# Filter rows of a spatially varying 3x3 filter made four times, in four groups of partitions

## The chip, the cores and the metric

The kernel runs on one NeuronCore of one Trainium2 chip. The metric is the device time of one execution in microseconds (us). All data are 32-bit floats. In the profile PE is TensorE, PEld its loading of weights, DVE is VectorE, ACT is ScalarE, POOL is GpSimd, and SP is the engine that issues most DMAs.

## The reference, cut to what matters

Eight images of 64 channels and 64x64 pixels go through four layers: a convolution block with attention over all pixels (layer 0), two blocks of shifted-window attention with an MLP (layer 1), a filter whose nine taps are computed from the data (layer 2), and a selective state-space scan in four directions with a normalisation and a multi-scale block behind it (layer 3). The change lies in layer 2:

```python
def filter_norm(f, axis):
    m = jnp.mean(f, axis=axis, keepdims=True)
    sd = jnp.std(f, axis=axis, keepdims=True, ddof=1)
    return (f - m) / (sd + 1e-10) * STD          # STD = sqrt(2)/3

s = jnp.einsum('bchw,tc->bthw', x, sw) + sb[None, :, None, None]
s = filter_norm(s, axis=1)                       # nine values per pixel
...
cf = filter_norm(cf, axis=2)                     # nine values per channel
xp = jnp.pad(x, ((0, 0), (0, 0), (1, 1), (1, 1)))
out = jnp.zeros_like(x)
for idx in range(9):
    i, j = idx // 3, idx % 3
    out = out + xp[:, :, i:i+H, j:j+W] * s[:, idx:idx+1] * cf[:, :, idx, None, None]
a = jnp.where(out >= 0, out, 0.1 * out)
y = conv_general_dilated(a, w2, (1, 1), ((0, 0), (4, 4)), ...)   # 1x9 along a row
return x + y + b2
```

## The kernel before, in words

Two images at a time lie on the 128 partitions (64 channels each), with their 4096 pixels along the free dimension, in eight chunks of 512 pixels (`NCH = 8`, `CH = 512`). So there are four pairs of images.

The program (`tile_kernel`, end of the listing) first runs the front of pair 0 alone: layers 0, 1, 2 and the inputs of the scan (`_Direct.front`). Then `scans(p, ...)` runs the scans of pair p, and beside them, in small portions, the back of pair p-1 and the front of pair p+1. Those portions are Python generators: each `yield` carries a cost written by hand (2.3 for a tap of layer 2, 14 for the end of a chunk), and after every scan step as many portions are drawn as keep the front in step with the scans. After the fourth pair's scans its back runs alone. The order of the instructions in each engine's queue is fixed when the program is built; an engine takes its instructions in that order and waits where a semaphore asks for it. A second path (`_Net.layer0` to `layer3`) handles inputs out of range and isn't entered with these data; it shares some constants with the first.

A scan step is: two DMAs that spread rows of B and C over the partitions; one product on POOL (L1687); two exponentials on ACT (L1707) into PSUM; two scans on DVE (L1710); the products with C on POOL (L1721, or L1723 with half of them on DVE, L1724); and two matmuls with the identity on PE (L1737), of two passes each, that add the result to `y`. The product tile `v` has six buffers, so POOL's L1687 of a later step waits until the matmuls L1737 of an earlier one have read it.

Layer 2 in the first path (L1501 to L1551) does this for every chunk:

- L1515: one matmul turns the 128 channel rows into `p_m`, 18 rows (nine centred filter values for each of the two images). L1517 squares them on ACT, L1519 sums the squares over nine with a matmul (`var9`), L1522 to L1525 make 1/(sd + 1e-10) on ACT with logarithms and exponentials, and L1527 makes the filter rows `f` on DVE, 18 partitions by 512.
- For each of the nine taps, L1532 is a matmul with an 18x128 table (`pick`) that spreads the two rows of this tap over the 128 partitions (`pb`, a PSUM bank); L1535 on DVE multiplies the shifted image by the channel's filter value and by `pb` (`tap`, three buffers); L1536 adds it to `acc` with an identity matmul over all 128 rows.
- L1542 and L1543 apply the leaky ReLU, L1546 does the 1x9 convolution as nine matmuls into `py`, and L1549 adds the result to X.

Every 32-bit matmul appears as two weight loads and two passes in the trace, so one tap is two passes of L1532 and two of L1536. `acc` and `py` share one PSUM bank (tag `acc`, `bufs=1`), so the `acc` of the next chunk starts only when L1549 has read `py`, while up to three `pb` and `tap` of that chunk can be made ahead. Banks for `pb`, `p_m` and `p_v` come from a pool of three, or from two pools in turn while the front of pair 0 runs alone (`bank`, L1179).

The constants are packed on the host (`_pack`) into six arrays. `load` (L239) fetches an array with one DMA on ACT's queue: arrays 0 and 1 at the start, 2 (`TEMP`) for a moment during `prepare`, 5 (`TABLES`, the tables of layer 2, first 18 rows only) at the start of every layer 2. `prepare` (L308 to L316) multiplies `swbd` by `cen9` to get `swc`, and `cen9` by `sb` to get `sbc`. `channel_filters` (L802) uses the table `cw2T` in 36 small passes (L818) once per layer 2 and gives the channel's filter values `cf`.

Of the kernel before, what the change touches and what calls it, by code (L numbers as in the profile page):

```python
# [9 lines left out]
F32 = mybir.dt.float32  # L10
AF = mybir.ActivationFunctionType
ALU = mybir.AluOpType
# [66 lines left out]

GENERAL = ("xpT", "dtT", "alog", "rpb0", "rpb1", "maskh", "maskv", "norm1_b0", "norm1_b1", "qb0", "qb1", "kb0", "kb1", "vb0", "vb1", "pb0", "pb1", "f1b0", "f1b1", "norm2_b0", "norm2_b1", "smask")
TEMP = ("swbd", "ds")
TABLES = ("cw2T", "pick")
TEMPW = ("xr", "drT", "alogs", "rpbT0", "rpbT1", "maskq", "b_all", "smask_t")


def _pack(w):
# [62 lines left out]
    e9 = np.eye(TAPS, dtype=np.float32)  # L151
    put("swbd", _blockdiag(f["sw"]))
    put("sb", _dup(_col(f["sb"])))
    put("cen9", _blockdiag(e9 - np.float32(1.0 / TAPS)))
    put("var9", _blockdiag(np.full((TAPS, TAPS), 1.0 / (TAPS - 1), np.float32)))
    put("cw1T", _dup(f["cw1"].T))
    mid = f["cw1"].shape[0]
    put("cb1", _col(f["cb1"]))
    put("cw2T", f["cw2"].reshape(C, TAPS, mid).transpose(2, 1, 0))
    pick = np.zeros((2 * TAPS, TAPS, P), np.float32)  # L160
    for im in range(2):
        for t in range(TAPS):
            pick[TAPS * im + t, t, 64 * im : 64 * im + 64] = np.sqrt(2.0) / 3
    put("pick", pick)
    put("cb2", _dup(f["cb2"].reshape(C, TAPS)))
    put("gmask", np.repeat(np.eye(2, dtype=np.float32) / L, 64, axis=0))
    w2 = f["w2"][:, :, 0, :]
# [41 lines left out]
    temp = [x for x in items[n_first:] if x[0] in TEMP]  # L209
    tempw = [x for x in items[n_first:] if x[0] in TEMPW]  # L210
    keep = [x for x in items[n_first:] if x[0] not in GENERAL + TEMP + TEMPW + TABLES]
    tables = [(n, sh, a[0 : 2 * TAPS]) for n, sh, a in items if n in TABLES]
    packs, layout = [], []
    for g, part in enumerate((items[:n_first], keep, temp, tempw, late, tables)):
        packs.append(np.ascontiguousarray(np.concatenate([x[2] for x in part], axis=1)))
# [10 lines left out]
class _Net:  # L226
# [45 lines left out]
    def prepare(self):  # L272
        nc, w, const = self.nc, self.w, self.const
        self.eps = const.tile([P, 5], F32, name="eps", tag="eps")
        for i, e in enumerate((LN_EPS, CN_EPS, BN_EPS, 1e-37, 1e-10)):
            nc.gpsimd.memset(self.eps[:, i : i + 1], e)
        eps_bn = self.eps[:, 2:3]

        bn1 = w["bn1"]
        sc = const.tile([P, 2, C], F32, name="bn1sc", tag="bn1sc")  # L280
        self.bn_fold((sc[:, 0, :], sc[:, 1, :]), bn1[:, 0, :], bn1[:, 1, :], bn1[:, 2, :], bn1[:, 3, :], eps_bn)
        self.w1a = const.tile([65, C], F32, name="w1a", tag="w1a")
        nc.vector.tensor_tensor(self.w1a[0:64, :], w["w1T"][0:64], sc[0:64, 0, :], ALU.mult)
        nc.vector.tensor_copy(self.w1a[64:65, :], sc[64:65, 1, :])

        self.w1bd = const.tile([P, P], F32, name="w1bd", tag="w1bd")
        nc.gpsimd.memset(self.w1bd, 0.0)
        for im in range(2):
            lo = slice(64 * im, 64 * im + 64)
            nc.vector.tensor_tensor(self.w1bd[lo, lo], w["w1T"][lo], sc[lo, 0, :], ALU.mult)  # L290
        self.b1row = const.tile([1, 2, C], F32, name="b1row", tag="b1row")
        nc.vector.tensor_copy(self.b1row, sc[0:1, 1, :].unsqueeze(1).to_broadcast([1, 2, C]))
        self.ones = const.tile([P, P], F32, name="ones", tag="ones")
        nc.gpsimd.memset(self.ones, 1.0)
        self.sums = const.tile([P, B // 2, 2, 32], F32, name="sums", tag="sums")

        bn = w["bn23"]
        self.bn23 = const.tile([P, 4], F32, name="bn23", tag="bn23")
        for i in range(2):
            self.bn_fold(  # L300
                (self.bn23[:, 2 * i : 2 * i + 1], self.bn23[:, 2 * i + 1 : 2 * i + 2]),
                *[bn[:, 4 * i + k : 4 * i + k + 1] for k in range(4)],
                eps_bn,
            )

        nr = 2 * TAPS

        self.swc = const.tile([P, nr], F32, name="swc", tag="swc")  # L308
        self.sbc = const.tile([nr, 1], F32, name="sbc", tag="sbc")
        with self.tc.tile_pool(name="psf", bufs=1, space=PSUM) as ps:  # L310
            pw = ps.tile([P, nr], F32, name="pswc", tag="pswc")
            nc.tensor.matmul(pw, lhsT=w["swbd"], rhs=w["cen9"], start=True, stop=True)
            nc.scalar.activation(self.swc, pw, AF.Copy)
            pb = ps.tile([nr, 1], F32, name="psbc", tag="psbc")
            nc.tensor.matmul(pb, lhsT=w["cen9"], rhs=w["sb"], start=True, stop=True)
            nc.scalar.activation(self.sbc, pb, AF.Copy)  # L316
        self.dsum = const.tile([P, 1], F32, name="dsum", tag="dsum")
        nc.vector.tensor_reduce(self.dsum, w["ds"], AX.X, ALU.add)
# [523 lines left out]
    def layer2(self, X):  # L842
# [5 lines left out]
        with ExitStack() as st:  # L848
# [7 lines left out]
            for c in range(NCH):  # L856
                cols = slice(c * CH, (c + 1) * CH)

                pm = ps.tile([nr, CH], F32, name="ps_m", tag="mm")
                nc.tensor.matmul(pm, lhsT=self.swc, rhs=X[:, cols], start=True, stop=True)  # L860
                q = wk.tile([nr, CH], F32, name="q2", tag="q2")
                nc.scalar.activation(q, pm, AF.Square, bias=self.sbc)
                pv = ps.tile([nr, CH], F32, name="ps_v", tag="pv")
                nc.tensor.matmul(pv, lhsT=w["var9"], rhs=q, start=True, stop=True)

# [3 lines left out]
                nc.scalar.activation(d, d, AF.Ln, bias=self.eps[0:nr, 4:5])  # L869
                nc.scalar.activation(d, d, AF.Exp, scale=-1.0)  # L870
                f = wk.tile([nr, CH], F32, name="f2", tag="f2")
                nc.vector.scalar_tensor_tensor(f, pm, self.sbc, d, ALU.add, ALU.mult)

                acc = ps.tile([P, 8, 64], F32, name="acc", tag="acc", bufs=1)
                for t in range(TAPS):
# [272 lines left out]
class _Direct:  # L1148
# [352 lines left out]
    def layer2(self, X):  # L1501
        nc, tc, w, net = self.nc, self.tc, self.w, self.net
        XP = self.padded("XP")
        for c in range(NCH):
            nc.scalar.activation(self.rows(XP, c), self.img(X[:, c * CH : (c + 1) * CH]), AF.Copy)
            yield 1
        nr = 2 * TAPS
        with tc.tile_pool(name="w2", bufs=2) as wk:
            net.load(wk, (5,))
            cf = net.channel_filters(X, wk, self.pf, "f")  # L1510
            for c in range(NCH):
                x = X[:, c * CH : (c + 1) * CH]

                pm = self.bank("p_m", (nr, CH))
                nc.tensor.matmul(pm, lhsT=net.swc, rhs=x, start=True, stop=True)  # L1515
                q = wk.tile([nr, CH], F32, name="q2", tag="q2")
                nc.scalar.activation(q, pm, AF.Square, bias=net.sbc)  # L1517
                pv = self.bank("p_v", (nr, CH))
                nc.tensor.matmul(pv, lhsT=w["var9"], rhs=q, start=True, stop=True)  # L1519

                d = wk.tile([nr, CH], F32, name="d2", tag="d2")
                nc.scalar.activation(d, pv, AF.Ln, bias=net.eps[0:nr, 3:4])  # L1522
                nc.scalar.activation(d, d, AF.Exp, scale=0.5)
                nc.scalar.activation(d, d, AF.Ln, bias=net.eps[0:nr, 4:5])
                nc.scalar.activation(d, d, AF.Exp, scale=-1.0)  # L1525
                f = wk.tile([nr, CH], F32, name="f2", tag="f2")
                nc.vector.scalar_tensor_tensor(f, pm, net.sbc, d, ALU.add, ALU.mult)  # L1527

                acc = self.total("acc", (P, 8, 64))
                for t in range(TAPS):  # L1530
                    pb = self.bank("pb", (P, 8, 64))
                    nc.tensor.matmul(pb, lhsT=w["pick"][:, t, :], rhs=f, start=True, stop=True)  # L1532
                    src = XP[:, 8 * c + t // 3 : 8 * c + t // 3 + 8, t % 3 : t % 3 + 64]
                    tap = wk.tile([P, 8, 64], F32, name="tap", tag="tap", bufs=3)
                    nc.vector.scalar_tensor_tensor(tap, src, cf[:, t : t + 1], pb, ALU.mult, ALU.mult)  # L1535
                    nc.tensor.matmul(acc, lhsT=w["ident"], rhs=tap, start=(t == 0), stop=(t == TAPS - 1))  # L1536
                    yield 2.3
                a = wk.tile([P, 8, 72], F32, name="act", tag="act")
                nc.vector.memset(a[:, :, 0:4], 0.0)
                nc.vector.memset(a[:, :, 68:72], 0.0)  # L1540
                t1 = wk.tile([P, 8, 64], F32, name="t1", tag="t1", bufs=1)
                nc.scalar.activation(t1, acc, AF.Copy)  # L1542
                nc.vector.scalar_tensor_tensor(a[:, :, 4:68], acc, 0.1, t1, ALU.mult, ALU.max)  # L1543
                py = self.total("py", (P, 8, 64))
                for t in range(TAPS):
                    nc.tensor.matmul(  # L1546
                        py, lhsT=w["w2bd"][:, t, :], rhs=a[:, :, t : t + 64], start=(t == 0), stop=(t == TAPS - 1)
                    )
                nc.vector.scalar_tensor_tensor(  # L1549
                    self.img(x), py, w["b2"], self.img(x), ALU.add, ALU.add  # L1550
                )  # L1551
                yield 14
# [336 lines left out]
```

## Time and profile before

| what | value |
|---|---|
| median of 3 runs | 14022.91 us |
| lowest and highest | 14009.71 and 14023.95 us |
| the profiled execution's own time | 14012.53 us |
| its span, first to last instruction | 14010.7 us |
| mean granted TensorE clock | 0.862 |
| PE, DVE, ACT, POOL busy | 11364.2, 8425.0, 7041.2, 8178.9 us |
| PE's passes of L1532, all | 576, 331.6 us |
| PE's passes of L1536, all | 576, 403.5 us |
| layer 2 of pair 0 (alone), from its first L1532 to its last L1549 | 1409.5 to 1732 us |
| layer 2 of pairs 1, 2, 3 (beside scans) | 4081 to 4468, 7295 to 7659, 10654 to 11017 us |

A row of the groups and of the timeline has the line of the kernel, the engine, the operation, output<-inputs, shapes, and how often; times are in us, mean durations in ns. In the timeline the first two columns are start and length, and neighbouring instructions of one kind are merged ("x6" is six of them). The passes of a matmul overlap at their ends, so the distance from start to start says what a pass costs, rather than its own length. The table of windows gives, for each stretch, its length, then the busy time of PE, PEld, DVE, ACT and POOL (with the number of instructions), the granted TensorE clock (1.00 is full), the share of the DMA engines and GB/s.

### The profile page before, as it was taken

What the parts mean: (1) busy time and instruction counts of PE and PEld (TensorE: products, weight loads), DVE (VectorE), ACT (ScalarE), POOL (GpSimd) and SP (SyncE); (2) the same over time, 40 slices, a digit from 0 to 9 for tenths busy, and PEclk for the clock granted to TensorE, in tenths of its full rate; (3) what the DMA queues carried; (4) which work ended last, traced back from release to release, by engine and by line L of the source; (5) the groups of instructions that cost most, each with busy time, mean ns of one, the idle gap of its engine ahead of it and who ended that gap; (6) DMA issues with size and microseconds to landing.
All of it is one profiled execution on the core that took longest, in us unless ns stands there. A gap on an engine that the chain in (4) does not pass through costs nothing. (4 is left out here: it accounts for less than half of the span.)

```text
span 14010.7 us, 141613 instructions
## 1 busy us (share of the span) xinstructions
PE 11364.2 (81%) x46358; PEld 4240.7 (30%) x46358; DVE 8425.0 (60%) x9763; ACT 7041.2 (50%) x15460; POOL 8178.9 (58%) x4111
## 2 busy tenths in 40 slices
PE   9888979978888669988889667997998866666665
PEld 2255222234433222224433222223443222222221
DVE  0222254477766874356675767337666677997875
ACT  5533156556544645555553645555554554454442
POOL 0000046578767765556665685457666688878982
PEclk9966789989889789998899788998888878888887
DMA  0000044456555754445554675335544577878882
GB/s 17 1 1 2 6 163 162 159 185 226 195 181 189 246 195 149 135 154 176 176 177 160 227 248 172 131 132 189 173 163 166 183 253 259 273 250 275 276 273 97
DMA packets 705499, 2379.23 MB, mean 170 GB/s; under 512 B 81060, under 2 KB 81188, under 8 KB 703980
## 3 DMA queue, kind: packets, MB, share of 16 engines
q1 hardware_dynamic: 681024, 2315.57, 48.9%
q10 hardware_dynamic: 23724, 54.50, 1.0%
q8 instruction: 367, 6.01, 0.2%
q14 instruction: 384, 3.15, 0.1%
HBM read 2269.08 MB, written 100.66 MB: 169 GB/s over the span
## 5 line engine op out<-in xcount | busy, mean ns | idle before, releaser
L1687 POOL TENSOR_TENSOR vd<-B,du 128x1024 f32<-128x1024 f32 x2048 | 4841.8, 2369 | 3920.1 <-DMA B<-rows 2103.0
L1737 PE MATMUL yd<-vd,pack 128*128 128x512 f32 x8192 | 4625.9, 695 | 1265.4 <-POOL vd L1721 449.5
L1710 DVE TENSOR_TENSOR_SCAN hd<-dad,carry,vd 128x512 f32<-128x512 f32 x2464 | 3093.2, 1271 | 1146.2 <-ACT dad L1707 669.9
L1707 ACT ACTIVATE dad<-du,As 128x512 f32<-128x512 f32 x4096 | 2718.4, 680 | 1017.3 <-DVE hd L1710 701.9
L1737 PEld LDWEIGHTS yd<-vd,pack 128*128 128x128 f32 x8192 | 1624.1, 215 | 3956.6 <-issue 1863.1
L1721 POOL TENSOR_TENSOR vd<-hd,C 128x1024 f32<-128x1024 f32 x768 | 1811.7, 2359 | 1324.0 <-DVE hd L1710 695.7
L1723 POOL TENSOR_TENSOR vd<-hd,C 128x512 f32<-128x512 f32 x1280 | 1637.0, 1280 | 317.9 <-DVE hd L1710 230.0
L1277 ACT ACTIVATE e<-s 128x512 f32<-128x512 f32 x2048 | 1199.2, 591 | 1030.1 <-PE s L1271 1028.6
L1710 DVE TENSOR_TENSOR_SCAN dad<-dad,carry,vd 128x512 f32<-128x512 f32 x1120 | 1427.6, 1275 | 126.5 <-POOL vd L1687 77.5
L1271 PE MATMUL s<-X 64*128 64x512 f32 x4096 | 1343.5, 647 | 105.5 <-ACT e L1277 105.3
L1263 PE MATMUL po<-e,VT 128*64 128x512 f32 x4096 | 1155.4, 631 | 19.0 <-ACT e L1277 19.0
L1718 ACT ACTIVATE carry<-hd 128x1 f32<-128x1 f32 (+1 forms) x1792 | 357.3, 201 | 1225.9 <-DVE hd L1710 1215.5
L1724 DVE TENSOR_TENSOR vd<-dad,C 128x512 f32<-128x512 f32 x1280 | 860.9, 673 | 72.7 <-ACT carry L1718 62.4
L1425 PEld LDWEIGHTS w_av<-vals,w_e 64*64 64x64 f32 x16384 | 630.9, 163 | 204.5 <-ACT w_e L1415 99.4
L1425 PE MATMUL w_av<-vals,w_e 64*64 64x9 f32 x16384 | 658.6, 218 | 38.2 <-ACT w_e L1415 38.0
L1271 PEld LDWEIGHTS s<-X 64*128 64x128 f32 x4096 | 363.5, 187 | 1052.4 <-issue 823.7
L1710 DVE TENSOR_TENSOR_SCAN hd<-dad,vd 128x512 f32<-128x512 f32 x352 | 420.1, 1211 | 191.7 <-ACT dad L1707 88.3
L1748 DVE TENSOR_TENSOR Y<-Y,yd 128x512 f32<-128x512 f32 x128 | 124.8, 975 | 661.3 <-PE yd L1737 661.1
L1718 ACT ACTIVATE carry<-dad 128x1 f32<-128x1 f32 x1120 | 189.5, 169 | 616.6 <-DVE dad L1710 614.4
L1415 ACT ACTIVATE w_e<-w_e 128x512 f32<-128x512 f32 x512 | 310.8, 627 | 360.7 <-DVE w_e L1410 239.4
L1410 DVE TENSOR_TENSOR w_e<-w_s,bias 128x512 f32<-128x512 f32 x512 | 328.8, 682 | 236.3 <-PE w_s L1398 235.3
L1263 PEld LDWEIGHTS po<-e,VT 128*64 128x64 f32 x4096 | 212.9, 136 | 824.6 <-issue 581.0
(247 smaller groups left out, 11150.5 us busy)
## 6 DMA issues: line engine op xcount, KB each, us to landing
B<-rows SPq DMA_DIRECT2D x2048, 512.0 KB, 5.0
C<-rows SPq DMA_DIRECT2D x2048, 512.0 KB, 4.5
xs<-xt SPq DMA_DIRECT2D x128, 256.0 KB, 2.9
xs<-xc SPq DMA_DIRECT2D x128, 256.0 KB, 3.4
xc<-xcv ACTq DMA_DIRECT2D x64, 256.0 KB, 3.8
zs<-z ACTq DMA_DIRECT2D x64, 256.0 KB, 3.8
xt<-XT ACTq DMA_DIRECT2D x32, 512.0 KB, 7.8
rows<-bc SPq DMA_DIRECT2D x256, 64.0 KB, 2.0
```

Source lines behind the costliest of these rows:

```text
L1263: nc.tensor.matmul(po[half[im]], lhsT=VT[:, t, half[im]], rhs=es[im], start=(t == 0), stop=(t == 31))
L1271: nc.tensor.matmul(ss[im], lhsT=at(half[im], t), rhs=X[half[im], jc * CH : (jc + 1) * CH], start=True, stop=True)
L1277: nc.scalar.activation(e, ss[im], AF.Exp, scale=C**-0.5, accum_out=parts[:, im, t, jc : jc + 1])
L1425: nc.tensor.matmul(self.av[half[im], x % 4 + j, h, :], lhsT=es[h // 4][half[im], j, h % 4, :], rhs=V[half[im], x + j, h, :], start=True, s ...
L1687: self.nc.gpsimd.tensor_tensor(v, st["B"], dx.to_broadcast([P, 2, TD]), ALU.mult)
L1707: nc.scalar.activation(da, u["du"][:, 0], AF.Exp, scale=net.As[:, k, n : n + 1])
L1710: nc.vector.tensor_tensor_scan(along(to), along(da), along(v[:, j]), first, ALU.mult, ALU.add)
L1718: nc.scalar.activation(cs, ends, AF.Copy)
L1721: st["w"] = nc.gpsimd.tensor_tensor(v, h, CC, ALU.mult)
L1723: st["w"] = nc.gpsimd.tensor_tensor(v[:, 0], h[:, 0], CC[:, 0], ALU.mult)
L1724: nc.vector.tensor_tensor(v[:, 1], hs[1], CC[:, 1], ALU.mult)
L1737: m = nc.tensor.matmul(y, lhsT=w["ident"], rhs=st["v"][:, j], start=(n == 0), stop=(n == NST - 1))
```

## The change

The filter rows `f` are made four times. `cen9` becomes 128 columns wide, four copies of the 18 columns, each padded to 32, so that `swc` has 128 columns, `sbc` 128 rows, and `p_m`, `q`, `d` and `f` 128 partitions: rows 32g to 32g+17 hold copy g, and the 14 rows after each are zero in `p_m`. The 18x18 matrix `var9` is replaced by a 128x128 matrix `var94` with four copies on its diagonal. The table `pick` (18 rows, nine taps of 128 columns) is replaced by `picks` (128 rows, three of 128 columns), where tap t lies in rows 32(t % 4) and columns block t // 4; the matmul of tap t then reads rows 32(t % 4) to 32(t % 4)+17 of both `picks` and `f`. The number of instructions is the same. `TABLES` is now loaded with all 128 rows (`cw2T`, `picks`, `var94`), `cen9` moves to the array loaded for a moment in `prepare`, and `pick` to the array of the path that isn't entered, which takes slices of `swc` and `sbc`.

```diff
-GENERAL = ("xpT", ...)
-TEMP = ("swbd", "ds")
-TABLES = ("cw2T", "pick")
+GENERAL = ("pick", "xpT", ...)
+TEMP = ("swbd", "ds", "cen9")
+TABLES = ("cw2T", "picks", "var94")
...
-    put("cen9", _blockdiag(e9 - np.float32(1.0 / TAPS)))
+    cen9 = np.pad(_blockdiag(e9 - np.float32(1.0 / TAPS)), ((0, 0), (0, 32 - 2 * TAPS)))
+    put("cen9", np.tile(cen9, (1, 4)))
...
+    n9 = 2 * TAPS
+    pick, four, picks = np.zeros((n9, TAPS, P)), np.zeros((P, P)), np.zeros((P, 3, P))
+    for t in range(TAPS):
+        for im in range(2):
             pick[TAPS * im + t, t, 64 * im : 64 * im + 64] = np.sqrt(2.0) / 3
+        picks[32 * (t % 4) : 32 * (t % 4) + n9, t // 4] = pick[:, t]
+    var9 = items[[x[0] for x in items].index("var9")][2]
+    for g in range(4):
+        four[32 * g : 32 * g + n9, 32 * g : 32 * g + n9] = var9[0:n9]
     put("pick", pick)
+    put("picks", picks)
+    put("var94", four)
...
-    tables = [(n, sh, a[0 : 2 * TAPS]) for n, sh, a in items if n in TABLES]
+    tables = [x for x in items if x[0] in TABLES]
...
-        self.swc = const.tile([P, nr], F32, name="swc", tag="swc")
-        self.sbc = const.tile([nr, 1], F32, name="sbc", tag="sbc")
+        self.swc = const.tile([P, P], F32, name="swc", tag="swc")
+        self.sbc = const.tile([P, 1], F32, name="sbc", tag="sbc")
...
-                pm = self.bank("p_m", (nr, CH))
+                pm = self.bank("p_m", (P, CH))
                 nc.tensor.matmul(pm, lhsT=net.swc, rhs=x, start=True, stop=True)
-                q = wk.tile([nr, CH], F32, name="q2", tag="q2")
+                q = wk.tile([P, CH], F32, name="q2", tag="q2")
                 nc.scalar.activation(q, pm, AF.Square, bias=net.sbc)
-                pv = self.bank("p_v", (nr, CH))
-                nc.tensor.matmul(pv, lhsT=w["var9"], rhs=q, start=True, stop=True)
+                pv = self.bank("p_v", (P, CH))
+                nc.tensor.matmul(pv, lhsT=w["var94"], rhs=q, start=True, stop=True)
...
-                f = wk.tile([nr, CH], F32, name="f2", tag="f2")
+                f = wk.tile([P, CH], F32, name="f2", tag="f2")
                 nc.vector.scalar_tensor_tensor(f, pm, net.sbc, d, ALU.add, ALU.mult)

                 acc = self.total("acc", (P, 8, 64))
                 for t in range(TAPS):
+                    g = slice(32 * (t % 4), 32 * (t % 4) + nr)
                     pb = self.bank("pb", (P, 8, 64))
-                    nc.tensor.matmul(pb, lhsT=w["pick"][:, t, :], rhs=f, start=True, stop=True)
+                    nc.tensor.matmul(pb, lhsT=w["picks"][g, t // 4, :], rhs=f[g], start=True, stop=True)
```

More of the change, by code (lines that the diff above doesn't have):

```diff
@@ L78, in _window_tables @@
     return rpi, kinds
-GENERAL = ("xpT", "dtT", "alog", "rpb0", "rpb1", "maskh", "maskv", "norm1_b0", "norm1_b1", "qb0", "qb1", "kb0", "kb1", "vb0", "vb1", "pb0", "pb1", "f1b0", "f1b1", "norm2_b0", "norm2_b1", "smask")
-TEMP = ("swbd", "ds")
-TABLES = ("cw2T", "pick")
+GENERAL = ("pick", "xpT", "dtT", "alog", "rpb0", "rpb1", "maskh", "maskv", "norm1_b0", "norm1_b1", "qb0", "qb1", "kb0", "kb1", "vb0", "vb1", "pb0", "pb1", "f1b0", "f1b1", "norm2_b0", "norm2_b1", "smask")
+TEMP = ("swbd", "ds", "cen9")
+TABLES = ("cw2T", "picks", "var94")
 TEMPW = ("xr", "drT", "alogs", "rpbT0", "rpbT1", "maskq", "b_all", "smask_t")
@@ L159, in _pack @@
     put("cw2T", f["cw2"].reshape(C, TAPS, mid).transpose(2, 1, 0))
-    pick = np.zeros((2 * TAPS, TAPS, P), np.float32)
-    for im in range(2):
-        for t in range(TAPS):
+    n9 = 2 * TAPS
+    pick, four, picks = np.zeros((n9, TAPS, P)), np.zeros((P, P)), np.zeros((P, 3, P))
+    for t in range(TAPS):
+        for im in range(2):
             pick[TAPS * im + t, t, 64 * im : 64 * im + 64] = np.sqrt(2.0) / 3
+        picks[32 * (t % 4) : 32 * (t % 4) + n9, t // 4] = pick[:, t]
+    var9 = items[[x[0] for x in items].index("var9")][2]
+    for g in range(4):
+        four[32 * g : 32 * g + n9, 32 * g : 32 * g + n9] = var9[0:n9]
     put("pick", pick)
+    put("picks", picks)
+    put("var94", four)
     put("cb2", _dup(f["cb2"].reshape(C, TAPS)))
@@ L306, in prepare @@
         nr = 2 * TAPS
-        self.swc = const.tile([P, nr], F32, name="swc", tag="swc")
-        self.sbc = const.tile([nr, 1], F32, name="sbc", tag="sbc")
+        self.swc = const.tile([P, P], F32, name="swc", tag="swc")
+        self.sbc = const.tile([P, 1], F32, name="sbc", tag="sbc")
         with self.tc.tile_pool(name="psf", bufs=1, space=PSUM) as ps:
-            pw = ps.tile([P, nr], F32, name="pswc", tag="pswc")
+            pw = ps.tile([P, P], F32, name="pswc", tag="pswc")
             nc.tensor.matmul(pw, lhsT=w["swbd"], rhs=w["cen9"], start=True, stop=True)
             nc.scalar.activation(self.swc, pw, AF.Copy)
-            pb = ps.tile([nr, 1], F32, name="psbc", tag="psbc")
+            pb = ps.tile([P, 1], F32, name="psbc", tag="psbc")
             nc.tensor.matmul(pb, lhsT=w["cen9"], rhs=w["sb"], start=True, stop=True)
@@ L859, in layer2 @@
                 pm = ps.tile([nr, CH], F32, name="ps_m", tag="mm")
-                nc.tensor.matmul(pm, lhsT=self.swc, rhs=X[:, cols], start=True, stop=True)
+                nc.tensor.matmul(pm, lhsT=self.swc[:, 0:nr], rhs=X[:, cols], start=True, stop=True)
                 q = wk.tile([nr, CH], F32, name="q2", tag="q2")
-                nc.scalar.activation(q, pm, AF.Square, bias=self.sbc)
+                nc.scalar.activation(q, pm, AF.Square, bias=self.sbc[0:nr])
                 pv = ps.tile([nr, CH], F32, name="ps_v", tag="pv")
@@ L871, in layer2 @@
                 f = wk.tile([nr, CH], F32, name="f2", tag="f2")
-                nc.vector.scalar_tensor_tensor(f, pm, self.sbc, d, ALU.add, ALU.mult)
+                nc.vector.scalar_tensor_tensor(f, pm, self.sbc[0:nr], d, ALU.add, ALU.mult)
                 acc = ps.tile([P, 8, 64], F32, name="acc", tag="acc", bufs=1)
@@ L1512, in layer2 @@
                 x = X[:, c * CH : (c + 1) * CH]
-                pm = self.bank("p_m", (nr, CH))
+                pm = self.bank("p_m", (P, CH))
                 nc.tensor.matmul(pm, lhsT=net.swc, rhs=x, start=True, stop=True)
-                q = wk.tile([nr, CH], F32, name="q2", tag="q2")
+                q = wk.tile([P, CH], F32, name="q2", tag="q2")
                 nc.scalar.activation(q, pm, AF.Square, bias=net.sbc)
-                pv = self.bank("p_v", (nr, CH))
-                nc.tensor.matmul(pv, lhsT=w["var9"], rhs=q, start=True, stop=True)
-                d = wk.tile([nr, CH], F32, name="d2", tag="d2")
-                nc.scalar.activation(d, pv, AF.Ln, bias=net.eps[0:nr, 3:4])
+                pv = self.bank("p_v", (P, CH))
+                nc.tensor.matmul(pv, lhsT=w["var94"], rhs=q, start=True, stop=True)
+                d = wk.tile([P, CH], F32, name="d2", tag="d2")
+                nc.scalar.activation(d, pv, AF.Ln, bias=net.eps[:, 3:4])
                 nc.scalar.activation(d, d, AF.Exp, scale=0.5)
-                nc.scalar.activation(d, d, AF.Ln, bias=net.eps[0:nr, 4:5])
+                nc.scalar.activation(d, d, AF.Ln, bias=net.eps[:, 4:5])
                 nc.scalar.activation(d, d, AF.Exp, scale=-1.0)
-                f = wk.tile([nr, CH], F32, name="f2", tag="f2")
+                f = wk.tile([P, CH], F32, name="f2", tag="f2")
                 nc.vector.scalar_tensor_tensor(f, pm, net.sbc, d, ALU.add, ALU.mult)
```

## The prediction

> **What bounds the kernel now.** I read the page's busy shares first, then a table of windows over the four layers 2, which are all that the change touches.
>
> ```profile
> PE 11364.2 (81%) x46358; PEld 4240.7 (30%) x46358; DVE 8425.0 (60%) x9763; ACT 7041.2 (50%) x15460; POOL 8178.9 (58%) x4111
> ...
> 1409.50:1731.80 322.30, 308.46 (x466) 96.42 (x466) 70.67 (x107) 28.52 (x44) 0.00 (x0) 0.71 0.02 6
> 4081.00:4469.00 388.00, 363.09 (x721) 132.21 (x722) 232.33 (x266) 127.04 (x269) 236.03 (x115) 0.92 0.49 166
> 7295.30:7659.80 364.50, 339.95 (x659) 122.57 (x659) 191.77 (x224) 99.06 (x202) 180.71 (x88) 0.89 0.40 136
> 10654.50:11018.00 363.50, 341.38 (x659) 123.16 (x660) 192.03 (x224) 99.13 (x203) 180.71 (x88) 0.89 0.40 136
> ```
>
> The four stretches are 1438 us of the 14010.7. In each PE is busy 93 to 96% of the time, no other engine over 61%: PE sets the pace there, and its clock is only 0.71 in the first and 0.89 to 0.92 in the others. The waits say the same: in 7295 to 7658 us POOL stands 105.7 us on its L1687 for PE's L1737, which is queued behind layer 2's matmuls. Next the timeline of PE alone, in layer 2 of pair 0:
>
> ```profile
> 1456.56 2.84 PE L1532 MATMUL pb<-f,pack 18*128 18x512 f32 x6
> 1459.33 2.84 PE L1536 MATMUL acc<-tap,pack 128*128 128x512 f32 x6
> 1462.10 3.09 PE L1532 MATMUL pb<-f,pack 18*128 18x512 f32 x6
> ```
>
> Three `pb` matmuls in a row (six passes) take 2.77 us from start to start, as much as three full-height ones: though they use 18 rows, they stand one behind the other. Now the same view in layer 0, where neighbouring matmuls use different halves of the rows (L1271) or columns (L1263):
>
> ```profile
> 389.95 1.13 PE L1271 MATMUL s<-X 64*128 64x512 f32 x4
> 391.01 1.08 PE L1263 MATMUL po<-e,VT 128*64 128x512 f32 x4
> 392.02 0.70 PE L1271 MATMUL s<-X 64*128 64x512 f32 x2
> ```
>
> Two matmuls of two passes, also 512 wide, take 1.06 us together, as one alone would. Last, windows of 3.41 us with the clock, where the taps of pair 2 begin:
>
> ```profile
> 7304.77:7308.18 3.41, 3.41 (x8) 1.43 (x9) 2.12 (x3) 0.00 (x0) 0.00 (x0) 1.00 0.61 228
> 7308.18:7311.59 3.41, 3.41 (x5) 1.01 (x3) 0.13 (x1) 0.00 (x0) 0.00 (x0) 0.50 0.00 0
> 7311.59:7315.01 3.42, 3.42 (x8) 1.33 (x8) 1.71 (x3) 0.00 (x0) 0.00 (x0) 1.00 0.00 0
> 7315.01:7318.42 3.41, 3.41 (x5) 1.35 (x4) 0.54 (x1) 0.00 (x0) 0.00 (x0) 0.50 0.00 0
> ```
>
> The same windows for L1532 alone show 2.75 and 2.84 us of `pb` in the first and third, none in the others. A window filled with `pb` is followed by one at half clock, though PE was busy all through; a window filled with `acc` by one at full clock.
>
> **What the Trainium skill says.** "TensorE: Matmul & The Clock Gate", section Part 3: Packing small matmuls, has matmuls of 32 rows in distinct row groups run at once, four of them (512 wide) 3.07 times as fast as in series; the trace agrees for two halves of 64 rows, and shows nothing for quarters at full width. The same page, Part 1, gives clock windows of 3413 ns at half or full rate, set by recent activity; the windows above agree, and add that 18 busy rows weigh little. "TensorEngine Tiling (Array Packing)", section Key Properties, says that a change of tiling mode drains TensorE: a lone `pb` between two `acc` costs about what an `acc` costs, before and after.
>
> **The change part by part.**
>
> *Overlap.* It only acts where `pb` matmuls stand next to each other in PE's queue. Counting runs of L1532 between other matmuls in the timeline: pair 0 has 28 alone, 4 twos and 12 threes; pair 1 has 9, 12 and 13; pairs 2 and 3 have 9, 6 and 17 each. Adjacent taps always fall in different groups. I take this order as kept. A three costs six passes of 0.43 us now, two when fully overlapped, so 1.73 us less. But DVE's three taps (0.75 us, 0.82 from start to start) then come late: `pb` done at 1.1, taps done at 1.9, 2.7, 3.5, `acc` 0 starts at 1.9 and the three run to 4.55, where the period was 5.55. That is 0.95 us per three. For a two the same sum gives 0.8 us (of 0.87). Pair 0: 12 x 0.95 + 4 x 0.8 = 14.6 us, with nothing beside it to take it away. Pairs 1 to 3: 47 x 0.95 + 24 x 0.8 = 63.9 us. There the engines beside PE get tighter: in the steady pattern (two taps and one scan step per 5.5 us) DVE has 2 scans of 1.27, 0.42 for L1724 on average and two taps of 0.75, 4.5 us, which fills 4.7 us to 96%; POOL's step is 2.37 + 1.69 = 4.05. I take 70%, 44.7 us; ends 0.3 (19) and all.
>
> *Clock.* 10, 10, 9 and 11 windows at half clock in the four stretches follow one with at least four passes of `pb`; each loses 1.7 us of PE's work. After the change a three is busy in three groups for 1.1 us and `acc` follows, so no window holds `pb` alone. I let half of the 40 go: 20 x 1.7 = 34, at 70% 24 us. Ends: none, all 68; and below nothing, see the rivals. The long half-clock stretches of pair 0 (`pb` and `acc` in turns, 36 us each) stay.
>
> *Additions.* L1515 and L1519 load 128 columns where they loaded 18: 64 + 64 loads at about 190 ns (row L1546) for 98, half of them hidden by the pass before: 64 x 0.09 = 6 us on PE. ACT's and DVE's instructions on 128 partitions for 18: L1522 673 ns against 681 for the same operation on 128 (L1212), L1527 728 against 744 (L1327): 1 us in all. The table DMA grows from 121.5 KB to 128 x 1088 x 4 bytes, 544 KB. It is issued at 1394.3 and read by L818 at 1400.5 in pair 0; 8.6, 11.1 and 11.1 us later in the others. Packs of 424.5 and 1891 KB took 9 and 13 us to land at the start, 512 KB (`B<-rows`) 5.0. So pair 0 may wait 0 to 3 us once on PE, with p_v and the first `pb` queued behind; elsewhere the sum over X on DVE covers it. The wider `cen9` costs under 1 us at the start. I take 6 us, ends 2 and 12.
>
> Sum: -14.6 - 44.7 - 24 + 6 = -77 us on the profiled execution's 14012.5: 13935. The median stood 10 us above that execution, so 13946 for the median.
>
> **The rivals.**
>
> *Everything is won* (all passes and windows): 292 passes x 0.43 = 126, and 68, less 6: -188, 13835. For it: PE over 93% busy. Against it: DVE's chain of taps.
>
> *The gain is swallowed beside the scans*: DVE and POOL, at 96% and 86% of a shortened period, take over; 30% of the overlap and no clock: -14.6 - 19 + 6 = -28, 13995.
>
> *No overlap*: quarters at full width run in series, or a wait on a bank separates them. Then only the additions stay: +6, 14029. Against it: L1271 and L1263; for it: no quarter at full width in the trace.
>
> *Slower: the clock gate punishes the waiting.* PE now stands about 0.9 us per three for the taps; if this counts as idleness, more windows go to half clock, and all that PE does there, the scan's L1737 and the 18 passes of L1546 too, runs slower. Pairs 1 to 3 hold 0.90 x 1116 = 1004 us of full-clock work, 959 after the overlap; the change loses from a mean clock of 0.86 downwards. At 0.83 these stretches take 1155 us, +39; with pair 0 at no gain and 6 us of additions, +45: 14068 for the median. Against it: at 7321 to 7329 PE stays at full clock; windows fell to half with PE busy throughout, so rows weigh more than time.
>
> **How the numbers follow.** Forecast 0.50 (own range 13890 to 13990), everything won 0.13, swallowed 0.12, no overlap 0.09, slower clock 0.16. About 0.2%, 28 us, can be told from no change. Faster: 0.50 + 0.13 + half of 0.12 = 0.69; slower 0.16; same 0.15. The range 13840 to 14050 leaves out the far end of the won case and more than half of the slower one, under 0.2.
>
> **What would show it.** Right: runs of L1532 x6 about 1.1 us long, followed by a gap for L1535; L1536 starting on DVE's tap rather than on "issue"; windows in layer 2 of pairs 1 to 3 at a clock of 0.92 or more; these stretches 15 to 35 us shorter, layer 2 of pair 0 about 15. Wrong: x6 still 2.8 us apart; fewer neighbouring `pb` in another order of PE's queue; a clock below 0.86; or shorter layers 2 whose time comes back in the stretches after them, where DVE and POOL are busier.

## The result, and the profile after

The changed kernel takes 13922.82 us (median of 6 runs, 13913.8 to 13935.38) against 14016.31 us before (6 runs beside it, 13987.48 to 14039.42). The ratio is 0.9933, 95% interval 0.9920 to 0.9946: 0.5 to 0.8% faster. Its profiled execution took 13924.36 us.

The page and the table of windows of the changed kernel, over its own four layers 2, from the first `pb` to the last addition to X (columns as before; the line numbers of the changed kernel are about ten higher: `pb` is L1542, `tap` L1545, `acc` L1546, `py` L1556, the scan's sums L1747):

```profile
PE 11204.1 (80%) x46358; PEld 4196.8 (30%) x46358; DVE 8415.1 (60%) x9763; ACT 7038.9 (51%) x15460; POOL 8173.5 (59%) x4111
...
1407.30:1697.80 290.50, 262.83 (x467) 85.02 (x468) 68.61 (x107) 28.85 (x44) 0.00 (x0) 0.75 0.02 7
4032.60:4404.50 371.90, 323.25 (x719) 118.82 (x719) 229.73 (x265) 126.43 (x266) 235.97 (x115) 0.93 0.51 173
7252.10:7589.40 337.30, 290.49 (x657) 107.94 (x657) 188.52 (x224) 98.57 (x201) 180.62 (x88) 0.92 0.43 146
10578.80:10917.50 338.70, 290.03 (x657) 108.52 (x657) 188.65 (x224) 98.54 (x201) 180.53 (x88) 0.92 0.42 146
```

Measured from the same edges, the stretches before were 322.6, 386.9, 363.5 and 362.4 us, so they are 32.1, 15.0, 26.2 and 23.7 us shorter, 97.0 together. All the rest is 12584 us against 12575, 9 us longer. The span fell by 88 us, and the whole gain lies in the layers 2. The clock there rose from 0.71, 0.92, 0.89, 0.89 to 0.75, 0.93, 0.92, 0.92, and PE is now busy 86 to 90% of the time in place of 93 to 96%. The work of DVE, ACT and POOL in them is nearly the same as before.

The timeline of PE in the changed kernel, at a chunk of pair 0 whose taps stand as threes, and then at one where single `pb` and `acc` take turns:

```profile
1452.01 1.13 PE L1542 MATMUL pb<-f,pack 18*128 18x512 f32 x6
1453.98 2.84 PE L1546 MATMUL acc<-tap,pack 128*128 128x512 f32 x6 [0.83 <-DVE tap L1545]
1456.75 1.13 PE L1542 MATMUL pb<-f,pack 18*128 18x512 f32 x6
...
1480.25 2.07 PE L1542 MATMUL pb<-f,pack 18*128 18x512 f32 x4 [3.64 <-DVE f L1536]
1483.16 2.08 PE L1546 MATMUL acc<-tap,pack 128*128 128x512 f32 x2 [0.84 <-DVE tap L1545]
1485.17 2.07 PE L1542 MATMUL pb<-f,pack 18*128 18x512 f32 x2
1487.17 2.08 PE L1546 MATMUL acc<-tap,pack 128*128 128x512 f32 x2
```

Six passes of `pb` now take 1.13 us where they took 2.84; `acc` then waits 0.83 us for DVE's first tap, and a three comes every 4.74 us (1456.75 less 1452.01) where it came every 5.54. The turns are as they were, 2.0 us for each matmul at half clock, with PE busy throughout. Before, in the timeline of another chunk and the table of windows:

```profile
1494.66 2.07 PE L1532 MATMUL pb<-f,pack 18*128 18x512 f32 x2
1496.66 2.08 PE L1536 MATMUL acc<-tap,pack 128*128 128x512 f32 x2
...
1418.00:1440.00 22.00, 22.00 (x23) 5.49 (x22) 3.82 (x6) 0.00 (x0) 0.00 (x0) 0.50 0.00 0
```

The waits in layer 2 of pair 2 (who waited, for whom, us in total, times, longest) show PE waiting more for DVE's taps, and POOL less for PE's queue:

```profile
POOL vd L1697 <- PE yd L1747: 85.7, 20, 14.1
...
PEld acc L1546 <- DVE tap L1545: 62.7, 60, 3.7
```

Before, in the same layer 2:

```profile
POOL vd L1687 <- PE yd L1737: 105.7, 17, 19.5
...
PEld acc L1536 <- DVE tap L1535: 29.0, 34, 2.0
```

### The profile page after: what moved, and what is told of

Its sections match the earlier page's. It is cut to its first block, busy times and chain, and to the rows that moved or that the text cites. A ratio compares the mean times of both kernels' runs of the same rounds, so it can differ in the third digit from the quotient of the medians.

```text
span 13922.6 us, 141613 instructions
## 1 busy us (share of the span) xinstructions
PE 11204.1 (80%) x46358; PEld 4196.8 (30%) x46358; DVE 8415.1 (60%) x9763; ACT 7038.9 (51%) x15460; POOL 8173.5 (59%) x4111
## 5 line engine op out<-in xcount | busy, mean ns | idle before, releaser
L1747 PE MATMUL yd<-vd,pack 128*128 128x512 f32 x8192 | 4627.1, 695 | 1250.7 <-POOL vd L1731 451.2
L1747 PEld LDWEIGHTS yd<-vd,pack 128*128 128x128 f32 x8192 | 1628.5, 215 | 3931.4 <-issue 1846.7
```

What stands on the lines that cost most here:

```text
L1747: m = nc.tensor.matmul(y, lhsT=w["ident"], rhs=st["v"][:, j], start=(n == 0), stop=(n == NST - 1))
```

## The experiments

Each was timed beside the kernel before, with four runs (the change six, one group 20); ratios are to it, with the 95% interval. The columns on layer 2 come from each run's profile, from its first `pb` to its last addition to X; "half clock" is the time in these four stretches that the clock record gives at half rate.

The engines' queues of two groups have the order of the kernel before. In one group, full height, zero rows, zero weights, 66 rows and halves, pairs 0 and 1 keep it, but the first 100 us or so of layer 2 in pairs 2 and 3 stand in another order; two column halves and the threes have another order throughout. So what is read from pair 0 is free of the order in all but these last.

| kernel | ratio | layer 2 of pair 0, us | of pairs 1 to 3, us | half clock, us |
|---|---|---|---|---|
| before | | 322.6 | 1112.8 | 410 |
| the change | 0.9933 (0.9920 to 0.9946) | 290.5 | 1047.9 | 304 |
| one group | 0.9991 (0.9985 to 0.9998) | 315.1 | 1126.5 | 420 |
| two groups | 0.9933 (0.9916 to 0.9949) | 291.1 | 1045.4 | 291 |
| full height | 0.9864 (0.9848 to 0.9881) | 227.0 | 1040.6 | 88 |
| zero rows | 0.9874 (0.9858 to 0.9891) | 227.6 | 1039.8 | 86 |
| zero weights | 0.9877 (0.9861 to 0.9894) | 224.1 | 1039.8 | 73 |
| 66 rows | 0.9893 (0.9872 to 0.9915) | 230.0 | 1057.5 | 150 |
| halves | 0.9913 (0.9897 to 0.9930) | 290.0 | 1035.5 | 227 |
| two column halves | 0.9911 (0.9894 to 0.9927) | 232.6 | 1090.3 | 73 |
| threes | 0.9901 (0.9885 to 0.9918) | 243.2 | 1034.6 | 215 |
| full height, threes | 0.9900 (0.9883 to 0.9916) | 249.7 | 1044.0 | 109 |

### Is it the overlap? One group, two groups

```diff
-        picks[32 * (t % 4) : 32 * (t % 4) + n9, t // 4] = pick[:, t]
+        picks[32 * (t % 1) : 32 * (t % 1) + n9, t // 1] = pick[:, t]
...
-                    g = slice(32 * (t % 4), 32 * (t % 4) + nr)
+                    g = slice(32 * (t % 1), 32 * (t % 1) + nr)
...
```

> The change with all nine taps in the first group of rows; the filter rows are still made four times, and PE's queue has the same order. If the gain comes from pb matmuls that run at once (and from the clock that follows), it is gone: ratio to before 0.9995 to 1.0010, runs of six pb passes 2.8 us from start to start again. If it came from anything else in the change (operations on 128 partitions, the tables, where the arrays lie), the ratio stays near 0.993.

The timeline of PE in this kernel:

```profile
1456.08 2.84 PE L1542 MATMUL pb<-f,pack 18*128 18x512 f32 x6
1458.85 2.84 PE L1546 MATMUL acc<-tap,pack 128*128 128x512 f32 x6
```

The ratio is 0.9991, a little under the expected 0.9995 to 1.0010: nearly all of the gain is gone, the passes stand in series again, and the half-clock time is back at 420 us. So the gain hangs on the rotation of the groups. The interval (0.9985 to 0.9998) leaves a gain of about 0.1% that isn't explained. What the rest of the change costs in layer 2 is small: 1441.6 us for the four stretches against 1435.4 in one profile of each, and no cost shows in the timed runs.

With two groups in place of four (`t % 2`, `t // 2`):

> Taps take turns between two groups of rows, not four. In a three, the third pb then follows the first: 2.0 us in place of 1.1. If DVE's taps set the length of a three (pb ready at 1.1, third tap done at 3.5), two groups do nearly as well: the period of a three 4.7 to 4.9 us against 4.73, ratio to before 0.993 to 0.995. If what counts is how short PE's stay in pb is, about half of the gain remains: ratio 0.996 to 0.997.

Its timeline of PE:

```profile
1453.87 1.98 PE L1542 MATMUL pb<-f,pack 18*128 18x512 f32 x6
1455.84 2.84 PE L1546 MATMUL acc<-tap,pack 128*128 128x512 f32 x6
1458.61 1.98 PE L1542 MATMUL pb<-f,pack 18*128 18x512 f32 x6
```

Six passes take 1.97 us, the period is 4.74 us all the same, and the ratio is that of the change. DVE's taps set the length of a three. No gain of four groups over two can be seen here.

### Is it the clock? Full height, and what the rows must hold

```diff
-        picks[32 * (t % 4) : 32 * (t % 4) + n9, t // 4] = pick[:, t]
+        for g in range(4):
+            picks[32 * g : 32 * g + n9, t] = pick[:, t] / 4
...
-                    g = slice(32 * (t % 4), 32 * (t % 4) + nr)
...
-                    nc.tensor.matmul(pb, lhsT=w["picks"][g, t // 4, :], rhs=f[g], start=True, stop=True)
+                    nc.tensor.matmul(pb, lhsT=w["picks"][:, t, :], rhs=f, start=True, stop=True)
```

> Every pb matmul uses all 128 rows: the table has a quarter of the weight in each of the four groups, so the sum is the same. No two pb matmuls can overlap, and the order of PE's queue is the same. If the clock is set by how many rows are busy, the half-clock windows in the layers 2 go (372 us before, of which pair 0 has 147): pair 0 about 73 us shorter, pairs 1 to 3 together 50 to 110, ratio 0.987 to 0.991, faster than the change itself. If the clock follows PE's waiting or its switching between taps and sums instead, nothing is gained: ratio 1.000 and the half-clock windows stay.

The table of windows of this kernel, over its layers 2 of pairs 0 and 2:

```profile
1413.40:1640.40 227.00, 212.95 (x467) 90.18 (x468) 71.12 (x107) 28.85 (x44) 0.00 (x0) 0.95 0.02 8
...
7188.10:7524.40 336.30, 301.73 (x661) 124.84 (x661) 193.54 (x227) 101.59 (x207) 185.39 (x90) 0.96 0.45 151
```

Its timeline of PE, in pair 0, at runs of six and in the turns:

```profile
1451.26 2.74 PE L1542 MATMUL pb<-f,pack 128*128 128x512 f32 x6
1453.83 2.74 PE L1546 MATMUL acc<-tap,pack 128*128 128x512 f32 x6
...
1476.63 1.02 PE L1542 MATMUL pb<-f,pack 128*128 128x512 f32 x2
1477.48 1.02 PE L1546 MATMUL acc<-tap,pack 128*128 128x512 f32 x2
```

Nothing overlaps here, and it is faster than the change: the intervals of the two ratios are apart. Pair 0 gets 95.6 us shorter. The clock record puts its half-clock time at 184.8 us before and 21 us here (the expectation's 147, and its 372 for all four stretches where the record has 410, were too low); those 164 us are 82 us of PE's work. The other 14 us fit a second effect: the switch between `pb` and `acc` costs nothing now, runs of six come 2.57 us apart where they came 2.77. In pairs 1 to 3 half-clock time fell from 225 to 67 us, and the stretches are 72 us shorter, against 65 with the change, where both overlap and clock gain.

Two kernels ask what the rows must hold. In one, `cen9` and `var94` have one copy, so that rows 18 to 127 of table and `f` are zero; in the other only the table is zero there:

```diff
-    put("cen9", np.tile(cen9, (1, 4)))
+    put("cen9", np.pad(cen9, ((0, 0), (0, 96))))
...
+        picks[0:n9, t] = pick[:, t]
...
```

> As the full-height form, but the filter rows are made once: rows 18 to 127 of both the table and f hold zeros, and pb still reads all 128 rows. If the clock counts the rows that a matmul addresses, whatever they hold, this equals the full-height form: ratio to before 0.985 to 0.988, pair 0 near 229 us, few half-clock windows, and the fourfold copies were not needed. If it counts what the rows do (products that are not zero), the half-clock windows come back: ratio 0.994 to 1.000, pair 0 280 to 320 us.

> As the form before in this list, but f has four copies of the filter rows, and only the table is zero in rows 18 to 127, so that data stream through all rows and meet zero weights. Counting addressed rows: ratio 0.985 to 0.988 again. Counting data that move through the array: also near that. Counting products that are not zero: as the kernel with zeros in both, 0.994 to 1.000.

All three are alike: the clock follows the rows that a matmul addresses, whatever they hold. Four copies were not needed for this gain, only a matmul with 128 rows.

### Rows, or the changes between parts and the whole?

In the turns, TensorE changes at every matmul between a part of the array and the whole. Three kernels separate that from the number of rows: `pb` on 64 rows, lower and upper half by turns (two copies at half the weight, so neighbours overlap); on 66 rows of the zero-row form, which take more than half of the array; and as two matmuls of 64 columns with all 128 rows.

```diff
+                    g = slice(64 * (t % 2), 64 * (t % 2) + 64)
+                    nc.tensor.matmul(pb, lhsT=w["picks"][g, t, :], rhs=f[g], start=True, stop=True)
...
+                    nc.tensor.matmul(pb, lhsT=w["picks"][0:66, t, :], rhs=f[0:66], start=True, stop=True)
...
+                    for h in self.HALF:
+                        nc.tensor.matmul(pb[h], lhsT=w["picks"][:, t, h], rhs=f, start=True, stop=True)
```

> Each pb matmul uses 64 rows (two of the four copies, half the weight each), and neighbouring taps take turns between the lower and the upper half, so that two run at once. If busy rows set the clock and half of the array is enough, both gains come together: threes with a period near 4.7 us, pair 0's turns near 1.0 us per matmul in place of 2.0, ratio to before 0.984 to 0.987. If 64 rows are too few for the turns of pb and acc, pair 0's four chunks in turns stay at half clock and the ratio is 0.990 to 0.994.

> As the form with zeros in both operands, but pb reads rows 0 to 65 of the table and of f: two rows more than in the halves, nearly the same number of busy rows, and too many rows for half of the array. If the number of addressed rows sets the clock, pair 0's turns of pb and acc stay at half clock as with 64 rows: pair 0 270 to 295 us, ratio to before 0.990 to 0.994. If what holds the clock down in the turns is the change between a part of the array and the whole (the drains between pb and acc), it is gone: turns at about 0.86 us per matmul, pair 0 near 228 us, ratio 0.986 to 0.989.

> Full-height pb split into two matmuls of 64 columns (lower and upper half of the output's partitions), as layer 0 does for po: all rows busy, the two run at once, but TensorE still goes from parts of the array to the whole and back between pb and acc. The order of PE's queue is another (mostly four such matmuls, then two acc). If the changes between part and whole hold the clock down by themselves, pair 0 stays at half clock for 100 us and more and takes 270 to 295 us. If it is the share of busy rows together with them, the clock in the layers 2 is 0.95 or more and pair 0 takes 230 to 255 us; ratio to before 0.986 to 0.991.

PE's timeline in pair 0's turns with 64 rows:

```profile
1418.90 2.08 PE L1547 MATMUL acc<-tap,pack 128*128 128x512 f32 x2
1420.90 2.07 PE L1543 MATMUL pb<-f,pack 64*128 64x512 f32 x2
```

With 66 rows:

```profile
1419.09 1.02 PE L1545 MATMUL acc<-tap,pack 128*128 128x512 f32 x2
1419.95 1.02 PE L1541 MATMUL pb<-f,pack 66*128 66x512 f32 x2
```

With two column halves:

```profile
1415.96 1.94 PE L1543 MATMUL pb<-f,pack 128*64 128x512 f32 x8
1417.87 1.98 PE L1547 MATMUL acc<-tap,pack 128*128 128x512 f32 x4
```

The granted clock in such stretches, first with 64 rows, then with 66:

```profile
1418.00:1440.00 22.00, 22.00 (x24) 5.50 (x22) 4.48 (x6) 0.00 (x0) 0.00 (x0) 0.50 0.00 0
1417.00:1426.00 9.00, 9.00 (x23) 3.94 (x22) 3.74 (x5) 0.00 (x0) 0.00 (x0) 1.00 0.00 0
```

Two rows more, and a turn falls from 4.0 to 1.7 us: full clock, and no stall at the change from `pb` to `acc`. Taken alone this speaks for the changes as the cause, as the expectation had it. But with column halves there is a change every 1.9 us, as often as in the turns at half clock (every 2.0 us), and all rows are busy; pair 0 has only 5 us at half clock (the second case expected). So a change by itself doesn't hold the clock down.

What fits all of them is a count of passes weighted by their rows. A pass over 512 columns takes 0.43 us at full clock and 0.85 us at half, so a clock window of 3.41 us holds eight passes at full clock or four at half. Count a pass over r rows as r/128, and sum over a window:

| in one window | weighted passes | next window |
|---|---|---|
| turns with 18 rows, half clock, 4.0 us a turn | 1.9 | half |
| turns with 64 rows, half clock, 4.0 us a turn | 2.6 | half |
| turns with 66 rows, half clock, 3.4 us a turn | 3.0 | full |
| `acc` alone, half clock (7308.18 in the prediction's table) | 4.0 | full |
| two column halves and `acc`, full clock, each half counted as a pass | 11 | full |
| mostly `pb` with 18 rows, full clock (7304.77 there) | 2.3 | half |

The dividing line is near 3. This holds for all kernels. Counted from the records of PE's passes in the four layers 2 of all twelve traces, 4644 windows, a window under 3 is followed by half clock and one over 3 by full clock in all but 26, and 23 of the 26 lie within 0.2 of 3. Unweighted passes, that is how busy PE is, miss 267 even with the line where it fits them best. Counting only rows of `pb` that hold something other than zeros misses 131 in the same way. Taking 66 rows as the whole array misses 18 of the 377 windows of that kernel, where 66 as 66 misses one. So it is the addressed rows, times the passes, that set the clock of the next window here. With 66 rows the first case expected (rows set the clock, so the turns stay slow) didn't come, though rows do set it: it left out that without the stall more passes fit into a window. The stall acts on the clock too, but through the count.

The kernel of halves has 1035.5 us for pairs 1 to 3, as hoped; only pair 0's turns stay slow. Two column halves take 1090.3 us there, 50 more than full height at the same half-clock time; that kernel has twice as many `pb` passes and another order, and which of them costs the time isn't shown.

### Can the order be had better? Threes

```diff
+                for t0 in range(0, TAPS, 3):
+                    pbs, taps = [], []
+                    for t in range(t0, t0 + 3):
...
+                        pbs.append(pb)
+                    for t in range(t0, t0 + 3):
...
+                        taps.append(tap)
+                    for t in range(t0, t0 + 3):
+                        nc.tensor.matmul(acc, lhsT=w["ident"], rhs=taps[t - t0], start=(t == 0), stop=(t == TAPS - 1))
+                    yield 6.9
```

> The change with the taps written by threes (three pb, three taps, three sums), so that all of them stand as threes in PE's queue, where pair 0 had 28 single pb and pairs 1 to 3 had 9 each. If neighbours are what the overlap and the clock need, the four chunks of pair 0 that ran in turns at half clock lose 36 us each down to about 15: 70 to 85 us less in pair 0, 10 to 30 in the others together, ratio to before 0.984 to 0.988. If the turns are slow for another reason (banks, the chain of taps), pair 0 keeps its 291 us and the ratio stays near 0.993.

> Full-height pb and the taps written by threes. If the order by threes is what shortened pairs 2 and 3 (327 and 329 us, against 337 in the full-height form), those stay at 325 to 330 us, pair 0 is near 235 us (its f is made late in every chunk), and the ratio is 0.984 to 0.987 if nothing comes back later, 0.987 to 0.990 if the stretches after layer 2 grow by 14 us each as they did with threes and overlap.

Both missed: with overlap the ratio is 0.9901, above the expected 0.984 to 0.988; at full height pair 0 takes 250 us, not 235, and pairs 2 and 3 take 333 and 331 us, not 325 to 330. In the first every `pb` stands in a three, and pair 0 is 47 us shorter than with the change rather than 70 to 85. The timeline of PE in the first of them, at the start of a chunk of pair 0:

```profile
1436.15 2.08 PE L1544 MATMUL pb<-f,pack 18*128 18x512 f32 x6 [3.64 <-DVE f L1536]
1439.06 4.66 PE L1552 MATMUL acc<-tap,pack 128*128 128x512 f32 x6 [0.83 <-DVE tap L1549]
1443.65 1.13 PE L1544 MATMUL pb<-f,pack 18*128 18x512 f32 x6
```

In this order `f` is made only after `py` in every chunk; PE stands 3.64 us, the clock falls to half, and the first three costs 7.5 us in place of 4.7. Of the 61 us won in the four stretches against the change, 29 came back outside them in the profile (12614 us against 12584). With full height and threes they did not (12588), while the other kernels lie between 12563 and 12590; where those 29 us come from stays open. Neither beats the full height without threes.

## Why the prediction was right, point by point

The median stands at 13923 where 13946 was forecast, inside the likeliest case's own range. Forecast were 77 us, and 88 came in the profile. The mechanism was right, and the sum is close in part because errors cancel.

- *The order is kept.* Right: apart from swaps of single neighbouring matmuls outside layer 2, no engine's order differs, and the runs of `pb` are 28, 4, 12 and so on as counted.
- *Overlap.* Right in kind: quarters at full width do run at once. A three won 5.54 - 4.74 = 0.80 us, 0.95 was forecast: `acc` starts 1.97 us after the first `pb`, not 1.9, and six passes of `acc` with the switch take 2.77, not 2.65. Two groups show that DVE's taps are the limit, as the sum had it.
- *Clock.* The term was too small. Half-clock time fell by 106 us, 31 windows, which is 53 us of PE's work; 20 windows and 34 us were taken. That no three is followed by half clock in pair 0, and that the turns keep it, was forecast.
- *Pair 0.* Here the prediction was off by half: its sign of being right has layer 2 of pair 0 about 15 us shorter, and 32.1 were measured. The overlap gave 13 us (12 x 0.80 + 4 x 0.79), close to the 14.6 forecast; the rest is clock (half-clock time 184.8 to 143.7 us, 20 us of work), mostly because all ten windows that had followed `pb` went, not half of them. That 13 and 20 make 33 so nearly is in part chance: with one group, where nothing overlaps, pair 0 had 14 us less half-clock time than before and was 7.5 us shorter.
- *The share of it beside the scans.* 65 us were measured for pairs 1 to 3, out of 58 of overlap (47 x 0.80 + 24 x 0.85, a two going from 1.91 to 1.06 us) and 32 of clock: 72%, taken as 70%. The prediction had 64 and 25.5 (half of 30 windows) before the share. Overlap too large by 6 and clock too small by 6 cancel; the share itself was an estimate, and that it came true is luck as much as insight.
- *Additions.* Within the forecast: +6 us in the profile of one group, not seen in its timed runs. No cost of the larger table shows: L827 runs 6.2 us after the DMA's issue in pair 0, as L818 did.
- *The rivals.* "Swallowed" and "no overlap" fell, and so did "everything is won", since each three waits for DVE's first tap. The slower rival, a clock that punishes PE's waiting for taps, fell too: waits of 0.83 us in every three left the clock higher. "Rows weigh more than time" was the right reason against it, and the runs with full height turned it from an argument into a measurement.
- The Trainium skill, *"TensorE: Matmul & The Clock Gate"*, Part 3, has distinct row groups run at once; the trace now shows it for three quarters at full width, 1.13 us for 2.84.

What the prediction did not see is that the clock, not the overlap, was the larger thing to win: it said that rows weigh, but took the long half-clock stretches of pair 0 as given, and these are what a table of full height removes.

## What to carry to other kernels

Where TensorE is busy all the time and its clock is low, look at how many rows its matmuls address, and not only for idle time: in these traces a clock window needed about three full-height passes, of the eight that fit at full clock, for the next one to run at full clock. A short contraction that stands between full ones can be cheaper when it is padded to all 128 rows with zeros; overlapping it in row groups pays only where such matmuls are neighbours in the queue and what reads them can keep up.

## What the hardware showed unexpectedly

- TensorE, busy without a break, stayed at half clock for 37 us at a time when 18-row and 128-row matmuls took turns; padding the 18 rows with zeros to 128 brought it to full clock, and a turn of `pb` and `acc` from 4.0 to 1.7 us.
- The clock of the next window of 3.41 us followed the passes weighted by addressed rows, with the line near 3 of 8, in 4618 of 4644 windows; zeros count as rows, and 66 rows count as 66.
- Between 64 and 66 rows a turn of `pb` and `acc` went from 4.0 to 1.7 us.
- A run of six passes costs 2.77 us when its neighbours use another part of the array, and 2.57 when they don't.
